# Spreading query and key rows in narrower parts in the last attention layer of a four-layer kernel

## The chip, the cores and the metric

The kernel runs on one core of a Trainium2 chip. The metric is device time of one execution in microseconds (us); less is better. The engines are named as in the profile: PE is TensorE's matmul part and PEld its weight load, DVE is VectorE, ACT is ScalarE, POOL is GpSimd, SP is SyncE, which here only starts DMAs.

## The reference, cut to what matters

A sequence `x` of shape (4, 256, 256) passes through four layers. Each is `x + attention(layernorm(x), ctx)` and then `x + ffn(layernorm(x))`; the context `ctx` has 1601 rows of 256 for each of the four batches. Only the attention of layer 3 is touched, together with the feed-forward that is woven into it:

```python
def _L3_xattn_ref(x, context, Wq, Wk, Wv):        # 32 heads of 8 columns
    q = x @ Wq.T ; kv = interleave(context @ Wk.T, context @ Wv.T)
    q = _rmsnorm(q) ; k = _rmsnorm(k)             # t * rsqrt(mean(t*t) + 1e-6), per head
    attn = softmax(q k^T * 8 ** -0.5)             # 256 queries x 1601 keys, 32 heads
    return attn @ v
x = x + _L3_xattn_ref(_layernorm(x), ctx_2048, ...)
x = x + _L3_ffn_ref(_layernorm(x), ...)           # quantised to whole numbers, 256 -> 1024 -> 256
```

All of it is in float32, except the whole-number matmuls of the feed-forward.

## The kernel before, in words

The program is written engine by engine with Python generators: each `yield` ends a step, and the main loop of layer 3, in `l3`, takes one step of a side generator for each of its own. A scheduler then arranges each engine's instructions, so that the order on an engine is near the program's order, not the same; each engine then works through its instructions in that order.

A head has only 8 columns, so four heads are put on the PE at once, 32 rows apart. For a group `u` of four heads, `runs` (line 1966) takes the transposed rows, copies eight of them to each place by a shuffle on DVE (line 1973), splits the float into low and high bits with two masks on DVE, `hi` (line 1974) and `run` again (line 1975), which also blank the rows that don't belong to the head, and lets POOL subtract them into the matmul operand (line 1976). So a part costs three DVE instructions, in the order shuffle, mask, mask, and one on POOL. `spread` (line 1978) does that for one group: the queries (`qb`, 256 columns) and the keys (`kb`) in parts of 512 columns: 512, 512, 512 and 65. The shuffled rows `run3` have two buffers, the high bits `hi3` one, the operands `qb3` and `kb3` two. There are 8 groups in each of 4 batches: 32 groups, below called heads 0 to 31.

The main loop (from line 2087) goes over batches, groups and 7 pairs of key tiles (six pairs of 128 and one tile of 65 keys). In each step it issues the scores of a pair (8 matmuls, or 4 for the last), their exponentials on ACT (line 2001, two of 128x1024), the value products of the pair before (16 matmuls into the accumulator `o`, which has one buffer), and one step of the side generator `beside`. When a head's last products are done, DVE copies `o` to `os` (line 2103), and the next head's first value products wait for that copy. The spread of the next head begins in step 2 and goes on in steps 3 to 5 of the current one.

`beside` prepares the next batch: `l3_kv` makes keys and values (13 tiles: a matmul `b<-wkv,ctxT`, copies `kr` and `va`), squares and sums them, multiplies the keys by their norms in four products on POOL (line 1739, 4, 4, 4 and 1 tiles), yields three times, and transposes them on the PE (line 1750) into `kT`, which DVE copies (line 1751); `queries` does the same for the queries with squares in `l3_squares` (line 1762, scratch taken from the `run3` buffers). After that it runs the feed-forward of the batch before, in `ffn` (lines 1906 to 1964). All of these PE results go through one PSUM bank (`b`).

Of the kernel before, what the change touches and what calls it, by code (L numbers as in the profile page):

```python
# [24 lines left out]
P = 128  # L25
B = 4
# [34 lines left out]
class Kernel:  # L61
# [1644 lines left out]
    def l3_kv(self, b, st, early):  # L1706


        nc = self.nc
        ctxT = self.ctx3  # L1710
        pool = self.late3 if b % 2 else self.a3
        kr = st["kr"] = self.a3.tile([P, NM, D], F32, name="kr3")
        va = st["va"] = self.va3[b % 2]
        ss = st["ss"] = self.a3.tile([P, (NM + 2) * NH3 + 2], F32, name="ss3")
        for m in range(NM):
            copy = nc.scalar.copy if early() else nc.vector.tensor_copy
            tf = self.take()
            for k in range(2):
                self.mm(tf, ctxT[:, k, m * P : (m + 1) * P], self.wkv3[:, k, :], k == 0, k == 1)
            tp = tf.rearrange("p (h d c) -> p h d c", d=HD3, c=2)  # L1720
            copy(kr[:, m, :].rearrange("p (h d) -> p h d", d=HD3), tp[:, :, :, 0])
            for h in range(2):
                copy(
                    va[h][:, m, : 16 * (HD3 + 1)].rearrange("p (h e) -> p h e", e=HD3 + 1)[:, :, :HD3],
                    tp[:, h * 16 : (h + 1) * 16, :, 1],
                )
            if m in (4, 9, NM - 1):
                m0 = {4: 0, 9: 5}.get(m, 10)
                self.l3_squares(st, kr[:, m0 : m + 1, :], m0, early())
            if m == NM - 1 and b < B - 1:  # L1730
                self.ctx3 = self.load_ctxT(self.a3, b + 1, 1)
            yield
        if b == 0:
            nk = NM * NH3
            self.rstd(ss[:, :nk], ss[:, :nk], 1.0 / HD3, self.eps6)
        for m0, m1 in ((0, 4), (4, 8), (8, 12), (12, NM)):
            v = kr[:, m0:m1, :].rearrange("p m (h d) -> p (m h) d", d=HD3)
            f = ss[:, m0 * NH3 : m1 * NH3, None].to_broadcast([P, (m1 - m0) * NH3, HD3])
            nc.gpsimd.tensor_tensor(v, v, f, ALU.mult)
        yield  # L1740
        yield
        yield
        kT = st["kT"] = [pool.tile([P, MP], F32, name="kT3", bufs=2) for _ in range(2)]
        for m0 in range(0, NM, 4):
            for h in range(2):
                n = min(4, NM - m0)
                copy = nc.scalar.copy if early() else nc.vector.tensor_copy
                tp = self.take().rearrange("p (m k) -> p m k", k=P)
                for m in range(n):
                    nc.tensor.transpose(tp[:, m, :], kr[:, m0 + m, h * P : (h + 1) * P], self.ident)  # L1750
                copy(kT[h][:, m0 * P : (m0 + n) * P], tp[:, :n, :].rearrange("p m k -> p (m k)"))
                yield

    def l3_squares(self, st, v, m0, early, pool=None):

        n = v.shape[1]
        if pool:
            sq = pool.tile([P, 2, D], F32, name="sqq3", tag="run3")
        else:
            sq = self.a3.tile([P, 5, D], F32, name="sq3")  # L1760
        if early:
            self.nc.scalar.activation(sq[:, :n, :], v, AF.Square)
        else:
            self.nc.gpsimd.tensor_tensor(sq[:, :n, :], v, v, ALU.mult)
        self.nc.vector.tensor_reduce(
            st["ss"][:, m0 * NH3 : (m0 + n) * NH3], sq[:, :n, :].rearrange("p m (h d) -> p (m h) d", d=HD3),
            AX.X, ALU.add,
        )

    def l3(self, first):  # L1770
# [11 lines left out]
        with ExitStack() as es:  # L1782
# [37 lines left out]
            def queries(b, st, old=None, fill=lambda n: None):  # L1820

                ss = st["ss"]
                nk, nq = NM * NH3, (NM + 2) * NH3
                if old is not None:
                    stats(old)
                    nc.vector.tensor_scalar(
                        ss[:, nq:], mv[:, old, :, 1], float(HD3), HD3 * (1e-5 - 1e-6), ALU.mult, ALU.add
                    )  # L1830
                elif b:
                    nc.vector.memset(ss[:, nq:], 1.0)
                xn = normed(b, rs[:, b, :])
                fill(0)
                tp = bank().rearrange("p (k q t) -> p k q t", k=2, q=2)
                for k in range(2):
                    for q in range(2):
                        nc.tensor.transpose(tp[:, k, q, :], xn[:, q, k * P : (k + 1) * P], self.ident)
                xT = one.tile([P, 2, S], F32, name="xT3")
                nc.vector.tensor_copy(xT, tp.rearrange("p k q t -> p k (q t)"))  # L1840
                fill(1)
                yield
                tq = bank().rearrange("p (q d) -> p q d", q=2)
                for q in range(2):
                    for k in range(2):
                        self.mm(tq[:, q, :], xT[:, k, q * P : (q + 1) * P], self.wq3[:, k, :], k == 0, k == 1)
                qr = one.tile([P, 2, D], F32, name="qr3")
                nc.vector.tensor_copy(qr, tq)
                self.l3_squares(st, qr, NM, True, two)
                part = ss if b else ss[:, nk:nq]  # L1850
                nc.scalar.activation(part, part, AF.Sqrt, bias=self.eps6, scale=1.0 / HD3)
                nc.vector.reciprocal(ss[:, nk : nq + 2 if b else nq], ss[:, nk : nq + 2 if b else nq])
                qrv = qr.rearrange("p q (h d) -> p (q h) d", d=HD3)
                nc.vector.tensor_tensor(qrv, qrv, ss[:, nk:nq, None].to_broadcast([P, 2 * NH3, HD3]), ALU.mult)
                if b:
                    for c in range(0, nk, nk // 2):
                        nc.vector.reciprocal(ss[:, c : c + nk // 2], ss[:, c : c + nk // 2])
                fill(2)
                yield
                yield  # L1860
                qT = st["qT"] = two.tile([P, 2, S], F32, name="qT3")
                tp = bank().rearrange("p (h t) -> p h t", h=2)
                for h in range(2):
                    for q in range(2):
                        nc.tensor.transpose(tp[:, h, q * P : (q + 1) * P], qr[:, q, h * P : (h + 1) * P], self.ident)
                nc.vector.tensor_copy(qT, tp)
                yield
# [99 lines left out]
            def runs(out, v, u, n):  # L1967

                a = two.tile([P, 512], F32, name="run3")[:, : out.shape[1]]
                t = two.tile([P, 512], F32, name="hi3", bufs=1)[:, : out.shape[1]]
                nc.vector.stream_shuffle(a, v, [8 * u + k % 8 for k in range(32)])  # L1973
                nc.vector.tensor_scalar(t.bitcast(U32), a.bitcast(U32), low[:, n : n + 1], None, ALU.bitwise_and)  # L1974
                nc.vector.tensor_scalar(a.bitcast(U32), a.bitcast(U32), rest[:, n : n + 1], None, ALU.bitwise_and)  # L1975
                nc.gpsimd.tensor_tensor(out, a, t, ALU.subtract)  # L1976

            def spread(st, h, u):
# [1 line left out]
                q = two.tile([P, S], F32R, name="qb3")  # L1980
                k = two.tile([P, MP], F32R, name="kb3")
                yield k, q
                for c in range(0, MP, 512):
                    c1 = min(M, c + 512)
                    runs(k[:, c:c1], st["kT"][h][:, c:c1], u, 0)
                    if c == 0:
                        runs(q, st["qT"][:, h, :], u, 1)
                    yield

            def scores(k, q, ms):  # L1990
# [94 lines left out]
            for b in range(B):  # L2085
                nxt = {} if b else second
                side = beside(b, nxt)
                for n, (h, u) in enumerate(heads):
                    o = ps_o.tile([P, S], F32, name="o3")
                    now = kq  # L2090
                    for c, ms in enumerate(pairs):
                        e = scores(*now, ms)
                        if b + n == 0 and c < 2:
                            for _ in range(c + 1):
                                next(more)
                        if last is not None:
                            values(*last[:6])
                        if done is not None:
# [7 lines left out]
                        else:  # L2106
                            next(side, None)
                        last = (e, o, st["va"], h, u, ms, b)
                        if c == 2:
                            more = iter(())  # L2110
                            if n + 1 < len(heads):
                                more = spread(st, *heads[n + 1])
                            elif b + 1 < B:
                                while "qT" not in nxt:
                                    next(side)
                                more = spread(nxt, 0, 0)
                            kq = next(more, None)
                        if c >= 2:
                            next(more, None)
                for _ in side:  # L2120
                    pass
                st = nxt
# [175 lines left out]
```

## Time and profile before

| | |
|---|---|
| time, three runs | 2550.21 us median (2548.49 to 2553.97) |
| the profiled execution's own time | 2553.43 us |
| its span, first to last instruction | 2551.7 us |
| busy over the span | PE 92%, DVE 62%, ACT 51%, POOL 39% |
| mean granted PE clock over the span | 0.957 |

The loop of layer 3 runs from the first exponential at 1926 us to 2520 us. By batch:

| stretch, us | PE busy | DVE busy | ACT busy | POOL busy | granted clock |
|---|---|---|---|---|---|
| 1926 to 1956 (head 0) | 22.53 | 23.44 | 19.82 | 13.70 | 0.74 |
| 1956 to 2070 (heads 1 to 7) | 101.68 | 73.93 | 85.61 | 42.82 | 0.84 |
| 2070 to 2229 (heads 8 to 15) | 134.28 | 105.14 | 106.02 | 57.21 | 0.96 |
| 2229 to 2395 (heads 16 to 23) | 142.55 | 106.56 | 106.38 | 57.34 | 0.91 |
| 2395 to 2520 (heads 24 to 31) | 112.84 | 66.25 | 101.76 | 37.03 | 0.92 |

How to read it: "busy" of the PE includes matmuls that run slowly. The granted clock is 1.00 or 0.50 at any moment; a mean of 0.84 says that 32% of the stretch ran at half clock. In the lists of waits, a line is the waiting engine with tile and source line, an arrow, the engine and line that ended the wait, and then total us, number of waits and the longest.

### The profile page before, as it was taken

To read this page: it belongs to the slowest core of one execution; us is meant where nothing else is said; L and a number is where in the kernel's file an instruction comes from. 1 tells how busy PE (TensorE), PEld (TensorE's weight loads), DVE (VectorE), ACT (ScalarE), POOL (GpSimd) and SP (SyncE) were. 2 spreads that over 40 slices of the span, in tenths; PEclk is the share of its full clock that TensorE was granted. 3 is DMA by queue.
4 is the path that set the end of the run, shared out by engine and by line. 5 is a ranking of instruction groups with operands and counts; after the bars stand their busy time and mean duration, and the time that the engine had idled before them with its cause. 6 is when DMAs were issued, how large, how long until landed. Compare 5 with 4: busy or idle time off the path is not lost.

```text
span 2551.7 us, 44647 instructions
## 1 busy us (share of the span) xinstructions
PE 2354.8 (92%) x15959; PEld 1434.9 (56%) x15959; DVE 1592.4 (62%) x3552; ACT 1298.8 (51%) x2996; POOL 1005.5 (39%) x1677
## 2 busy tenths in 40 slices
PE   8989997899899999999999999989997888897897
PEld 5778876667545555555555555555553433433443
DVE  5443534843577777777777777763327756657664
ACT  3234444533654545444545454433336766756775
POOL 2015645213355555555555555541114333324330
PEclk9999998989999999999999999998998889998898
DMA  7165675634601111111111111004310100000000
GB/s 254 48 205 165 174 149 169 200 94 139 219 27 48 48 48 48 48 48 48 48 48 48 48 48 48 10 14 164 126 56 28 34 1 28 4 3 2 5 6 5
DMA packets 96516, 188.29 MB, mean 74 GB/s; under 512 B 15449, under 2 KB 64345, under 8 KB 95098
## 3 DMA queue, kind: packets, MB, share of 16 engines
q1 hardware_dynamic: 80150, 146.50, 17.3%
q0 software_dynamic: 10416, 28.46, 4.9%
q10 hardware_dynamic: 5732, 10.49, 1.4%
q8 instruction: 130, 2.13, 0.4%
q14 instruction: 88, 0.72, 0.1%
HBM read 137.29 MB, written 48.11 MB: 73 GB/s over the span
## 4 chain that ended last, share of the span: by engine, by line
PE 70%; DVE 14%; POOL 5%; issue 4%; ACT 3%; DMA 2%; another core or an unknown queue 1%; SPq 0%; ACTq 0%; POOLq 0%; DVEq 0%
PE o L79 21%; PE s L79 18%; PE f2gu L79 3%; POOL kb L1976 3%; PE f1gu L79 2%; PE acc L79 2%; PE tpq L79 2%; PE f0gu L79 2%; DVE run L1973 2%; PE b L79 2%; PE fill L1260 2%; PE tpkv L79 2%; PE av L79 2%; DVE hi L1974 2%; PE f0y L79 1%
## 5 line engine op out<-in xcount | busy, mean ns | idle before, releaser
L1520 ACT ACTIVATE p<-s,nmsm 128x448 f32<-128x448 f32 (+1 forms) x512 | 326.5, 644 | 372.3 <-PE s L79 243.1
L2001 ACT ACTIVATE e<-s 128x1024 f32<-128x1024 f32 (+1 forms) x448 | 398.1, 968 | 172.1 <-PE s L79 171.5
L79 PE MATMUL o<-pT,va 128*128 128x256 f32 (+2 forms) x1920 | 430.2, 376 | 5.9 <-DVE pT L1561 4.3
L79 PE MATMUL s<-kT,qT 128*32 128x448 f32 (+1 forms) x4096 | 427.7, 556 | 7.9 <-ACT kT L1492 7.7
L79 PEld LDWEIGHTS o<-pT,va 128*128 128x128 f32 (+1 forms) x1920 | 344.1, 190 | 126.5 <-issue 86.2
L1555 POOL TENSOR_SCALAR p<-p,rm 128x448 f32<-128x448 f32 (+1 forms) x512 | 324.5, 655 | 6.3
L79 PE MATMUL o<-e,va 128*32 128x256 f32 (+1 forms) x3328 | 291.5, 420 | 19.9 <-DVE os L2103 18.5
L1516 DVE TENSOR_REDUCE nmsm<-s 128x2 f32<-128x896 f32 (+1 forms) x256 | 287.3, 1123 | 8.0
L1561 DVE STREAM_TRANSPOSE pT<-p 128x896 f32<-128x896 f32 (+1 forms) x256 | 270.6, 1110 | 4.8 <-POOL p L1555 4.1
L79 PEld LDWEIGHTS s<-kT,qT 128*32 128x32 f32 x4096 | 120.5, 109 | 259.8 <-issue 238.3
L1976 POOL TENSOR_TENSOR kb<-run,hi 128x512 fp32r<-128x512 f32 (+1 forms) x128 | 137.0, 1070 | 290.9 <-DVE run L1975 154.4
L1548 POOL TENSOR_TENSOR rm<-em,tot 32x8 f32<-32x8 f32 x256 | 54.5, 213 | 396.2 <-DVE tot L1545 384.9
L79 PEld LDWEIGHTS o<-e,va 128*32 128x32 f32 (+1 forms) x3328 | 103.9, 115 | 119.6 <-ACT e L2001 25.4
L79 PE MATMUL s<-qb,kb 32*128 32x256 f32 (+1 forms) x1664 | 133.4, 351 | 16.5 <-ACT e L2001 14.1
L1513 DVE TENSOR_TENSOR s<-s,mask 128x128 f32<-128x128 f32 (+1 forms) x256 | 84.1, 330 | 98.8 <-PE s L79 90.7
L79 PEld LDWEIGHTS s<-qb,kb 32*128 32x128 f32 (+1 forms) x1664 | 78.8, 193 | 112.0 <-issue 72.9
L1974 DVE TENSOR_SCALAR hi<-run,low 128x512 uint32<-128x512 uint32 (+2 forms) x160 | 69.7, 436 | 114.7 <-POOL kb L1976 99.8
L1260 PE MATMUL fill<-wkc_early,ctxT 128*128 128x256 f32 (+1 forms) x444 | 109.6, 398 | 9.0 <-ACT va_early L1268 6.7
L475 POOL DMA_INDIRECT f0xr<-f0xd,f0src x95 | 90.9, 957 | 68.3 <-PE f0y L79 23.6
L1520 ACT ACTIVATION_READ_ACCUMULATOR p<-s,nmsm 128x1 f32 x512 | 101.4, 198 | 0.0
L1260 PEld LDWEIGHTS fill<-wkc_early,ctxT 128*128 128x128 f32 (+1 forms) x444 | 86.3, 198 | 24.9 <-ACT va_early L1268 7.9
L1279 DVE TENSOR_REDUCE ss_early<-sq_early 128x4 f32<-128x512 f32 x64 | 37.0, 579 | 82.2 <-ACT sq_early L1278 64.4
(518 smaller groups left out, 3893.7 us busy)
## 6 DMA issues: line engine op xcount, KB each, us to landing
ctxT<-in_ctxT SPq DMA_DIRECT2D x9, 1664.0 KB
vd<-va_early SPq DMA_DIRECT2D x96, 128.0 KB
kd<-kT_early SPq DMA_DIRECT2D x48, 256.0 KB
kT<-kd SPq DMA_DIRECT2D x16, 768.0 KB
va<-vd SPq DMA_DIRECT2D x16, 768.0 KB
f0yd<-f0ys SPq DMA_DIRECT2D x95, 128.0 KB
wq<-in_l_wq SPq DMA_DIRECT2D x16, 512.0 KB
wo<-in_l_wo SPq DMA_DIRECT2D x16, 512.0 KB
```

The costliest lines, as they stand in the source:

```text
L79: self.nc.tensor.matmul(out, lhsT, rhs, start=start, stop=stop, **kw)
L475: nc.gpsimd.indirect_dma_start(out=t, out_offset=None, in_=xd[:, :], in_offset=bass.IndirectOffsetOnAxis(ap=src[:, n : n + 1], axis=0),)
L1260: ins = nc.tensor.matmul(tp[:rows, t, :], ctxT[u // NKV2][:, k, c0 : c0 + rows], w[u % NKV2][:, k, :], start=k == 0, stop=k == 1,)
L1513: nc.vector.tensor_tensor(sv, sv, mask[:, 2 * c : 2 * c + 2, : nt - CT, :].rearrange("p n t i -> p n (t i)"), ALU.add)
L1516: nc.vector.tensor_reduce(ms[:, 0, 2 * c : 2 * c + 2], s[:, :, : nt * 32], AX.X, ALU.max, negate=True)
L1520: nc.scalar.activation(p[:, n, : nt * 32], s[:, n, : nt * 32], AF.Exp, bias=ms[:, 0, e : e + 1], accum_out=ms[:, 1, e : e + 1],)
L1548: nc.gpsimd.tensor_tensor(r[32 * a : 32 * a + 32], e[:, a], tot, ALU.mult)
L1555: nc.gpsimd.tensor_scalar(p[:, n, : nt * 32], p[:, n, : nt * 32], r[:, e : e + 1], 1.0, ALU.mult, ALU.mult)
L1561: self.pin(nc.vector.transpose(pT[:, 2 * c : 2 * c + 2, :nt, :].rearrange("p n t i -> p n (t i)"), p[:, :, : nt * 32]))
L1974: nc.vector.tensor_scalar(t.bitcast(U32), a.bitcast(U32), low[:, n : n + 1], None, ALU.bitwise_and)
L1976: nc.gpsimd.tensor_tensor(out, a, t, ALU.subtract)
L2001: nc.scalar.activation(e[:kr, :, :n, :], s[t][:kr, :, :n, :], AF.Exp, scale=1.0 / math.sqrt(HD3))
```

## The change

It has four parts, all in layer 3. `spread` handles the queries first and then the keys in parts of 256 columns (six of 256 and one of 65), one in each of the seven steps of the head before, so that it begins in step 0; in the first head its own spread runs along, one part in each step. `run3` and `hi3` become 256 columns wide, with three buffers each. The squares of the queries are taken in two halves. For batches 1 to 3, `l3_kv` yields between its four norm products and once behind them, in place of three times behind them.

```diff
@@ l3_kv
         for m0, m1 in ((0, 4), (4, 8), (8, 12), (12, NM)):
+            if m0 and b:
+                yield
             v = kr[:, m0:m1, :].rearrange("p m (h d) -> p (m h) d", d=HD3)
             f = ss[:, m0 * NH3 : m1 * NH3, None].to_broadcast([P, (m1 - m0) * NH3, HD3])
             nc.gpsimd.tensor_tensor(v, v, f, ALU.mult)
-        yield
-        yield
-        yield
+        for _ in range(1 if b else 3):
+            yield
@@ l3_squares
-        if pool:
-            sq = pool.tile([P, 2, D], F32, name="sqq3", tag="run3")
-        else:
-            sq = self.a3.tile([P, 5, D], F32, name="sq3")
+        sq = pool.tile([P, 1, D], F32, name="sqq3", tag="run3", bufs=3) if pool else self.a3.tile([P, 5, D], F32, name="sq3")
@@ queries
-                self.l3_squares(st, qr, NM, True, two)
+                for q in range(2):
+                    self.l3_squares(st, qr[:, q : q + 1, :], NM + q, True, two)
@@ runs
-                a = two.tile([P, 512], F32, name="run3")[:, : out.shape[1]]
-                t = two.tile([P, 512], F32, name="hi3", bufs=1)[:, : out.shape[1]]
+                a, t = (two.tile([P, S], F32, name=x, bufs=3)[:, : out.shape[1]] for x in ("run3", "hi3"))
@@ spread
-                for c in range(0, MP, 512):
-                    c1 = min(M, c + 512)
+                runs(q, st["qT"][:, h, :], u, 1)
+                for c in range(0, MP, 2 * P):
+                    c1 = min(M, c + 2 * P)
                     runs(k[:, c:c1], st["kT"][h][:, c:c1], u, 0)
-                    if c == 0:
-                        runs(q, st["qT"][:, h, :], u, 1)
                     yield
@@ the main loop, after scores of step c
-                        if b + n == 0 and c < 2:
-                            for _ in range(c + 1):
-                                next(more)
+                        if c == 0:
+                            own = more
+                            more = None
+                            if n + 1 < len(heads):
+                                more = spread(st, *heads[n + 1])
+                            elif b + 1 < B:
+                                while "qT" not in nxt:
+                                    next(side)
+                                more = spread(nxt, 0, 0)
+                            if more is not None:
+                                kq = next(more)
+                        if b + n == 0:
+                            next(own, None)
+                        if more is not None:
+                            next(more)
...
-                        if c == 2:
-                            more = iter(())
...
-                            kq = next(more, None)
-                        if c >= 2:
-                            next(more, None)
```

## The prediction

> **What bounds the kernel now.** Every edit lies in layer 3's loop, 1926 to 2520 us, 18.6 us for each of 32 heads. I read the waits of PE, DVE and POOL in that stretch first:
>
> ```profile
> PE o L79 <- DVE os L2103: 18.5, 16, 2.2
> PE s L79 <- ACT e L2001: 14.1, 15, 3.0
> PE b L1750 <- DVE kT L1751: 13.5, 13, 2.6
> PE b L79 <- DVE va L1723: 8.2, 5, 3.1
> PE b L79 <- DVE g L1938: 6.7, 5, 1.6
> PE b L1750 <- POOL kr L1739: 5.4, 3, 2.6
> ...
> DVE hi L1974 <- POOL kb L1976: 99.8, 92, 5.4
> DVE hi L1974 <- POOL qb L1976: 14.7, 23, 0.8
> ...
> POOL kb L1976 <- PE s L79: 61.9, 15, 12.4
> ```
>
> PE idles 80 us in all, and most of it is for DVE copies. DVE itself stands still 114.5 us in `hi`, since that tile has one buffer and the next mask waits for POOL's subtract; the subtract in turn waits until PE has read the old `kb`. The timeline at the start of head 29 shows how this reaches PE:
>
> ```profile
> 2478.27 0.73 POOL L1976 TENSOR_TENSOR qb<-run,hi 128x256 fp32r<-128x256 f32 x1 [1.36 <-DVE run L1975]
> ...
> 2479.03 0.48 DVE L1974 TENSOR_SCALAR hi<-run,low 128x512 uint32<-128x512 uint32 x1 [0.85 <-POOL qb L1976]
> ...
> 2480.07 0.40 DVE L2103 COPY os<-o 128x256 f32<-128x256 f32 x1
> ...
> 2480.53 1.94 PE L79 MATMUL o<-e,va 128*32 128x256 f32 x16 [1.40 <-DVE os L2103]
> ```
>
> The accumulator was complete at 2478.0, but its copy stood behind a mask that waited for POOL. PE lost 1.40 us and then more, as the busy times by stretch show (the number behind POOL's is the granted clock):
>
> ```profile
> 2476.00:2478.00 2.00, 2.00 (x31) 0.85 (x30) 1.05 (x4) 1.28 (x3) 0.91 (x1) 1.00 0.00 0
> 2478.00:2480.00 2.00, 0.96 (x12) 0.54 (x8) 1.15 (x4) 2.00 (x3) 0.73 (x1) 0.95 0.00 0
> 2480.00:2482.00 2.00, 1.47 (x16) 0.59 (x16) 0.86 (x3) 1.32 (x2) 1.06 (x1) 0.50 0.04 8
> 2482.00:2484.00 2.00, 2.00 (x22) 0.99 (x18) 1.33 (x6) 0.09 (x1) 0.46 (x2) 0.50 0.00 0
> ```
>
> A short wait is followed by half clock. The five stretches of the table by batch make it 2 x (0.26 x 30 + 0.16 x 114 + 0.04 x 159 + 0.09 x 166 + 0.08 x 125) = 115 us at half clock. A pair of key tiles takes 1.9 us at full clock (products start at 2501.62, 2503.52, 2505.35), where ACT's two exponentials of 0.97 us are the limit, and 2.6 us at half (scores at 2483.01 and 2485.60): a microsecond at half clock loses 0.27 us, 31 us in all.
>
> **The parts and their costs.**
>
> *More, smaller parts.* 32 heads x (8 - 5) = 96 more parts: 288 DVE and 96 POOL instructions. By shape DVE's shuffle and masks take 730 + 482 + 483 = 1695 ns for 512 columns, 440 + 353 + 337 = 1130 for 256, 227 + 255 + 244 = 726 for 65. A head goes from 3 x 1695 + 1130 + 726 = 6.94 to 7 x 1130 + 726 = 8.64 us: 1.70 more, 54 us over the loop. POOL goes from 3 x 1.31 + 0.76 + 0.36 = 5.05 to 7 x 0.76 + 0.36 = 5.68, 20 us in all. POOL is busy 208 of 594 us, so its share is hidden. DVE is busy 375; its extra time is hidden where it now stands still (114.5 us), and bare where it is behind. Bounds: 0 and 54. I take 0.2 us a head for 31 heads, 6 us, since DVE had 3.6 us of blocked time per head to give. Without that cover it is the 54.
>
> *Three buffers.* The first wait moves from the second part's mask behind one subtract to the third key part's shuffle behind the queries' subtract. In the changed program's DVE order `os` still stands behind such shuffles: behind that of the sixth part (waiting for the third subtract) in 8 of 31 heads, behind the third to fifth elsewhere. From POOL's start, head 29's copy began at +4.44 us (2475.63 to 2480.07). The new chain is subtracts of 0.73 us, with shuffle, mask, mask between them: +3.9 to +4.3 behind the sixth part, +3.3 behind the fifth, +2.4 behind the fourth. So of the 18.5 us for `os` a third goes, -6; bounds 0 and -18.
>
> *Norm products apart, key transposes later.* In heads 0, 10 and 18 the four products hold POOL for 6.8 to 6.9 us (1739), with the transposes stuck in the middle of a head's products: PE waits 5.4 us for `kr`, then 13.5 us for the `kT` copies, which queue behind masks that wait for subtracts behind those products. In the new order no transpose comes before the third pair of the next head, and two key parts' subtracts go between the products. The `kr` wait goes, -5.4. The copies come at DVE's pace, 3.2 us a pair before (transposes at 2149.93 to 2162.80, four intervals), some 2.7 by my count of the new rows between two copies: -8; bounds 0 and -13.5. The extra `yield` moves transposes, query work and feed-forward one step on; SP's context load is issued with the last key tile, ahead of it, and the output DMAs are not waited for.
>
> *Beside the squares on POOL* (heads 9 and 17) PE waits 3.1 us for `va`. The chain there starts with a subtract of 0.73 instead of 1.28 and one shuffle less: 1.2 us each, -2.4.
>
> *The first head* pays. Its own parts now come one step ahead, and the second stands on DVE behind six adds (line 1169, 2.92 us), the third behind statistics and copies of 4.4 us. Before, one part served two pairs. Adding up the new DVE order I get the last pair 4 us later: +4, bounds 0 and +10. Halved squares add 0.06 us, four times.
>
> *The clock.* If a third of the late copies goes, a quarter of the half clock goes: 115 / 4 x 0.27 = -8; bounds 0 and -20. The Trainium skill, page "TensorE: Matmul & The Clock Gate", Part 1, says that the clock falls after an idle window of about 3.4 us. No wait here is that long, so by it this term is 0 and the sum 8 us smaller; the trace has the fall behind 1.40 us and decides.
>
> The sum: +6 - 6 - 5.4 - 8 - 2.4 + 4 - 8 = -20 us against 2553.4, so 2533.6. The profiled execution is 3.2 us above the median; the forecast for the median is 2530.
>
> **The rivals.**
>
> *DVE and POOL shut each other out* (slower). Before, the single buffer kept masks and subtracts apart; of 320 masks only six met a POOL instruction of over 0.6 us:
>
> ```profile
> 2092.33 2.31 POOL L1764 TENSOR_TENSOR sq<-kr 128x1280 f32<-128x1280 f32 x1
> 2092.40 2.40 DVE L1974 TENSOR_SCALAR hi<-run,low 128x256 uint32<-128x256 uint32 x1 [0.90 <-POOL kb L1976]
> ```
>
> A mask of 0.35 us took 2.40, ending with POOL's instruction. With three buffers, masks and subtracts run side by side. If every subtract holds up one mask for its 0.73 us, a head's DVE time grows by 1.70 + 8 x 0.73 = 7.5, less the 3.6 of waits. DVE now has 375 / 32 = 11.7 busy and 3.6 blocked of 18.6 us: 3.3 free, so 0.6 us a head is bare, 20 us. Of the gains (-30 without the first head) half would go with it: 2550 + 20 + 4 - 15 = 2559. It decides once a head's subtracts hold up masks for more than about 5 us. For it: the row above. Against: shuffles don't meet this (0.739 beside POOL, 0.729 alone), and a held mask waits on average half a subtract. The Trainium skill, "SBUF — State Buffer", section "Who interferes with whom", has the same rule, an exclusive lock between such DVE instructions and GpSimd; the trace agrees.
>
> *The wait only moves* (no change). DVE stops at the third shuffle instead of the second mask, still until PE frees `kb`, and `os` is as late; the clock falls as before. Then -5.4 - 8 - 2.4 + 4 + 6 = -6, and half of the `kT` gain may go too: 2544 to 2552, say 2547. The lower end of my chain (+4.3 against +4.44) speaks for it.
>
> **How the numbers follow.** About 0.2%, 5 us, is what a measurement of this kernel can tell from no change. The forecast case has 0.52, its own range 2512 to 2543; the moved wait 0.20, half of it faster; the shut-out 0.28, almost all slower, to 2575 if it eats all gains. Faster 0.60, same 0.13, slower 0.27. The range, 2508 to 2568, leaves out the far ends of both.
>
> **What would show it.** Right: PE's wait for `kr` gone, those for `os` near 12 and `kT` near 5.5, DVE's waits for POOL well below 114.5, masks of 256 columns near 0.4 on the mean, mean clock in heads 1 to 7 over 0.88, head 0 longer. Wrong: 256-column masks of 0.6 or more on the mean, or `os` waits still near 18.

## The result and the profile after

The changed kernel takes 2524.30 us, median of 4 runs (2522.54 to 2526.93), against 2552.05 us for the kernel before beside it; the ratio is 0.9894 with a 95% interval of 0.9877 to 0.9911. A second comparison, on another chip, gave 0.9893 (0.9875 to 0.9911). So it is faster by 27.8 us, 1.1%, where the forecast was 20 us.

The profiled execution of after took 2525.47 us, with a span of 2523.8 us. Layer 3's loop, from its first exponential to its last, went from 595.3 us (1926.1 to 2521.4) to 565.0 us (1928.7 to 2493.7), 30.3 us less; its later start takes 2.6 us of that back, which is within what the start varies: the other runs in which the layers ahead take as long start it between 1922.8 and 1928.8 us. The same view of both loops (time, then busy us and instructions of PE, PE's weight load, DVE, ACT and POOL, the granted clock, DMA), before first:

```profile
1926.10:2521.40 595.30, 515.17 (x5438) 237.47 (x5436) 375.21 (x1070) 421.00 (x478) 208.10 (x239) 0.90 0.04 12
```
```profile
1928.70:2493.70 565.00, 500.62 (x5438) 237.29 (x5438) 419.17 (x1459) 421.20 (x482) 227.30 (x335) 0.93 0.04 13
```

PE has the same matmuls. It idles 80.1 us before and 64.4 after, 15.7 us less, and is busy 14.6 us less, as it runs fewer of them at half clock (115.9 us of the loop before, 78.5 after, added up from windows of 4 us). These two halves make the 30.3 us. DVE is busy 44 us more (the prediction's sum of durations gave 54) and POOL 19.

These are the waits that the prediction started from, now in after, first PE's and then DVE's (total us, number, longest):

```profile
PE o L79 <- DVE os L2112: 21.1, 17, 2.4
PE s L79 <- ACT e L1998: 11.7, 15, 3.0
PE b L79 <- DVE va L1723: 6.3, 4, 2.4
...
PE b L1751 <- DVE kT L1752: 3.9, 7, 1.2
PE b L79 <- DVE g L1937: 3.2, 7, 1.2
...
PE s L79 <- POOL kb L1974: 2.3, 3, 1.1
```
```profile
DVE run L1971 <- POOL qb L1974: 29.9, 19, 5.7
...
DVE run L1971 <- POOL kb L1974: 9.4, 30, 0.5
```

The wait for `kr` is gone, that for `kT` went from 13.5 to 3.9, `g` from 6.7 to 3.2. DVE's waits for POOL fell from 114.5 to 39.3 us, and stand at the shuffle now. The copy of the accumulator, `os`, did not follow: 18.5 before, 21.1 after.

### The profile page after: what moved, and what is told of

Read it like the earlier page. It is cut to its first block, busy times and chain, and to the rows that moved or that the text cites. A ratio compares the mean times of both kernels' runs of the same rounds, so it can differ in the third digit from the quotient of the medians.

```text
span 2523.8 us, 45207 instructions
## 1 busy us (share of the span) xinstructions
PE 2343.1 (93%) x15959; PEld 1436.2 (57%) x15959; DVE 1635.7 (65%) x3940; ACT 1299.5 (51%) x3000; POOL 1022.5 (41%) x1773
## 4 chain that ended last, share of the span: by engine, by line
PE 75%; DVE 14%; issue 4%; POOL 3%; DMA 3%; ACT 2%; SPq 0%; ACTq 0%; POOLq 0%; DVEq 0%
PE o L79 21%; PE s L79 18%; PE f2gu L79 3%; PE b L79 3%; PE f1gu L79 2%; PE fill L1260 2%; PE f0gu L79 2%; PE acc L79 2%; PE tpq L79 2%; PE tpkv L79 2%; PE av L79 2%; DVE hi L1972 2%; DVE run L1971 2%; PE f0y L79 1%; PE f2y L79 1%
## 5 line engine op out<-in xcount | busy, mean ns | idle before, releaser
L79 PE MATMUL o<-e,va 128*32 128x256 f32 (+1 forms) x3328 | 283.2, 410 | 27.1 <-DVE os L2112 21.1
L1974 POOL TENSOR_TENSOR kb<-run,hi 128x256 fp32r<-128x256 f32 (+1 forms) x224 | 155.8, 707 | 120.8 <-DVE run L1973 119.3
L1972 DVE TENSOR_SCALAR hi<-run,low 128x256 uint32<-128x256 uint32 (+1 forms) x256 | 100.4, 411 | 0.2
L1974 POOL TENSOR_TENSOR qb<-run,hi 128x256 fp32r<-128x256 f32 x32 | 25.9, 810 | 176.4 <-PE s L79 108.4
```

The source lines that it names most:

```text
L79: self.nc.tensor.matmul(out, lhsT, rhs, start=start, stop=stop, **kw)
```

## The experiments

Runs 5 to 7 and runs 8 to 11 were taken on two other chips, where the layers ahead of layer 3 take some 45 us less. So each run is read by its ratio to the kernel before on its own chip, and by its loop. "Half clock" is time of the loop at half clock, worked out as above.

| run | time, us | before beside it | ratio (95%) | loop, us | half clock, us |
|---|---|---|---|---|---|
| before | 2550.2 | | 1 | 595.3 | 116 |
| after | 2524.3 | 2552.1 | 0.9894 (0.9877 to 0.9911) | 565.0 | 79 |
| 1 products apart, alone | 2549.7 | 2552.9 | 0.9983 (0.9974 to 0.9991) | 589.3 | 113 |
| 2 after, products together | 2529.1 | 2552.9 | 0.9900 (0.9883 to 0.9916) | 570.6 | 99 |
| 3 after, old buffer counts | 2563.2 | 2552.9 | 1.0037 (1.0024 to 1.0051) | 601.2 | 113 |
| 4 after, old steps | 2517.1 | 2552.9 | 0.9858 (0.9841 to 0.9875) | 558.7 | 75 |
| 5 after, copy's place fixed | 2509.2 | 2505.5 | 1.0016 (1.0005 to 1.0028) | 597.2 | 126 |
| 6 run 4, copy's place fixed | 2519.6 | 2505.5 | 1.0054 (1.0041 to 1.0066) | 610.1 | 147 |
| 7 before, copy's place fixed | 2539.1 | 2505.5 | 1.0136 (1.0121 to 1.0151) | 623.9 | 160 |
| 8 after again | 2478.9 | 2507.9 | 0.9893 (0.9875 to 0.9911) | 562.5 | 70 |
| 9 after, two accumulators | 2479.4 | 2507.9 | 0.9888 (0.9869 to 0.9907) | 565.2 | 75 |
| 10 run 4, two accumulators | 2472.9 | 2507.9 | 0.9876 (0.9855 to 0.9896) | 560.9 | 82 |
| 11 before, two accumulators | 2508.2 | 2507.9 | 1.0007 (0.9993 to 1.0020) | 591.2 | 106 |
| 12 run 4, copy on ACT | 2524.0 | 2552.2 | 0.9895 (0.9877 to 0.9913) | 570.3 | 86 |

### 1. The norm products alone

```diff
@@ before: l3_kv
         for m0, m1 in ((0, 4), (4, 8), (8, 12), (12, NM)):
+            if m0 and b:
+                yield
...
-        yield
-        yield
-        yield
+        for _ in range(1 if b else 3):
+            yield
```

> The kernel before, with the fourth part of the change alone: the four norm products of the later keys one step apart, parts still 512 columns with two and one buffers. My theory gives this part the waits for the products and for the copies of the transposes: heads 10 to 12 and 18 to 20 were 57.8 and 60.0 us before and 54.4 and 54.5 after, 9 us together. So about 2542 us, 10 below before; the half clock stays near 116 us and DVE's waits for POOL near 110 us. Rival: the whole gain of 28 us comes from here, 2525 us. Other rival: DVE's blocked masks keep the copies late, so that the wait only moves from the products to the copies: 2550 us.

Measured: 3.2 us below before at the median, a loop 6.0 us shorter: between my 10 and the second rival's 2. Its waits of PE:

```profile
PE o L79 <- DVE os L2104: 23.5, 17, 2.4
...
PE b L1751 <- DVE kT L1752: 8.4, 9, 2.3
```

The wait for the products (5.4) is gone and `kT` fell by 5.1, but `os` rose from 18.5 to 23.5. About half of what this part takes away comes back at the copy of the accumulator: "the wait only moves" holds for this part, by half.

### 2. After, with the norm products together

```diff
@@ after: l3_kv
         for m0, m1 in ((0, 4), (4, 8), (8, 12), (12, NM)):
-            if m0 and b:
-                yield
...
-        for _ in range(1 if b else 3):
-            yield
+        yield
+        yield
+        yield
```

> The changed kernel, with the four norm products together again and three steps behind them. My theory: about 10 us above after, 2534 us, with PE's wait for the products back (5 us) and the waits for the copies of the transposes near 8 us; DVE's waits for POOL stay near 40 us outside heads 2, 10 and 18. Rival that all of the gain lies in the products: 2552 us. Rival that the narrow parts with three buffers hide them: 2525 us.

Measured: 2529.1 us, 4.8 us above after by the medians, a loop 5.6 us longer; the intervals of the two ratios overlap, so the time alone does not settle the size. PE's waits do show the exchange:

```profile
PE o L79 <- DVE os L2111: 14.2, 16, 1.6
...
PE b L1750 <- DVE kT L1751: 6.2, 12, 0.8
...
PE b L1750 <- POOL kr L1739: 2.6, 3, 0.9
```

With the products together `os` is 14.2 us. Apart, it is 21.1. So the buffers did shorten the waits for the copy, and the separate products lengthen them again. The timeline of after at the start of head 11 shows where (start, duration, engine and line, what; lines of one kind run together with their number):

```profile
2134.76 6.17 POOL L1741 TENSOR_TENSOR kr<-kr,ss 128x1024 f32<-128x1024 f32 x3 [1.75 <-ACT e L1998]
...
2137.73 3.35 DVE L1972 TENSOR_SCALAR hi<-run,low 128x256 uint32<-128x256 uint32 x2
2138.19 1.08 PE L79 MATMUL o<-e,va 65*32 65x256 f32 x8
...
2141.00 0.81 DVE L1973 TENSOR_SCALAR run<-run,rest 128x256 uint32<-128x256 uint32 x1
2141.73 0.41 DVE L2112 COPY os<-o 128x256 f32<-128x256 f32 x1
...
2142.20 1.08 PE L79 MATMUL o<-e,va 128*32 128x256 f32 x8 [1.97 <-DVE os L2112]
```

Three of the four products still ran back to back (one wait for ACT ahead of the first, none between). Two masks that take 0.7 us together at the median of such masks took 3.35 beside them, and the copy behind those masks was late for it: 1.97 us of PE's time. Heads 1 and 19 show the same, with 2.4 us each. This is the rival that DVE and POOL shut each other out, at three places of the loop and not throughout. The Trainium skill, "SBUF — State Buffer", section "Who interferes with whom", says that a DVE instruction in a two-port mode, which `tensor_scalar` can enter, and GpSimd take a shared port pair in turn, each for its whole instruction; the rows agree: in the single records each of the two masks ends 0.15 us behind one of the products.

### 3. After, with the old buffer counts

```diff
@@ after: runs
-                a, t = (two.tile([P, S], F32, name=x, bufs=3)[:, : out.shape[1]] for x in ("run3", "hi3"))
+                a, t = (two.tile([P, S], F32, name=x, bufs=c)[:, : out.shape[1]] for x, c in (("run3", 2), ("hi3", 1)))
@@ after: l3_squares
-        sq = pool.tile([P, 1, D], F32, name="sqq3", tag="run3", bufs=3) if pool else ...
+        sq = pool.tile([P, 1, D], F32, name="sqq3", tag="run3", bufs=2) if pool else ...
```

> The changed kernel with parts of 256 columns, but two buffers for the shuffled rows and one for the high bits. My theory: the extra DVE work of 54 us is hidden by the blocked time that the third buffer frees; without it DVE waits for POOL in each mask, over 120 us in all (39 after), the copies of the accumulator and of the transposes are as late as before or later, and the half clock is back near 116 us: 2545 to 2555 us, say 2548. Rival: the buffers do nothing, since DVE has 3 us free in each head anyway: 2525 us. Rival that side by side running of masks and subtracts costs more than it brings: masks of 256 columns back at 0.34 us and the time below 2520 us.

Measured: 2563.2 us, more than the 2545 to 2555 I expected, slower than before with its interval above 1, and a loop 36 us longer than after's. Its waits:

```profile
DVE hi L1972 <- POOL kb L1974: 93.9, 146, 0.9
PE o L79 <- DVE os L2112: 28.0, 19, 2.6
...
DVE hi L1972 <- POOL qb L1974: 16.8, 24, 2.1
PE b L79 <- DVE va L1723: 11.4, 9, 2.3
...
PE s L79 <- POOL kb L1974: 8.7, 5, 3.1
```

DVE waits 121 us for POOL in masks and shuffles, as before the change. Most waits of PE are longer: `os` 28.0 against 21.1, `va` 11.4 against 6.3, and that for the key parts `kb` 8.7 against 2.3. Of the 36 us, 30.7 are idle time of PE, and no single wait carries them; PE's busy time is 5.5 us more, though the half clock is back at 113 us. So narrow parts without the buffers cost more than they bring, and the added buffers (one for `run3`, two for `hi3`) are worth more than the whole gain, spread over many waits. More buffers with the wide parts were not tried, so the buffers' worth without the narrow parts stays open. The masks tell the price of running beside POOL (mean ns), first this run and then after:

```profile
L1972 DVE TENSOR_SCALAR hi<-run,low 128x256 uint32<-128x256 uint32 x222 | 86.8, 391 | 95.3 <-POOL kb L1974 77.6 <-POOL qb L1974 16.8
L1971 DVE STREAM_SHUFFLE run<-kT 128x256 f32<-128x256 f32 x190 | 83.7, 442 | 0.0
L1973 DVE TENSOR_SCALAR run<-run,rest 128x256 uint32<-128x256 uint32 x222 | 75.8, 342 | 0.7
```
```profile
L1972 DVE TENSOR_SCALAR hi<-run,low 128x256 uint32<-128x256 uint32 x224 | 91.0, 424 | 0.1
L1971 DVE STREAM_SHUFFLE run<-kT 128x256 f32<-128x256 f32 x192 | 82.7, 442 | 0.0
L1973 DVE TENSOR_SCALAR run<-run,rest 128x256 uint32<-128x256 uint32 x224 | 81.5, 378 | 0.6
```

### 4. After, with the steps of before

```diff
@@ after: spread
                     runs(k[:, c:c1], st["kT"][h][:, c:c1], u, 0)
-                    yield
+                    if c % 512 or c1 == M:
+                        yield
@@ after: the main loop, which becomes that of before
-                        if c == 0:
-                            own = more
...
-                        if b + n == 0:
-                            next(own, None)
-                        if more is not None:
-                            next(more)
+                        if b + n == 0 and c < 2:
+                            for _ in range(c + 1):
+                                next(more)
...
+                        if c == 2:
+                            more = iter(())
...
+                        if c >= 2:
+                            next(more, None)
```

> The changed kernel with parts of 256 columns and three buffers, but issued as before: two key parts in a step, from the third step of the head on (the queries still first), and in the first head its own parts ahead by the old rule. My theory: the steps themselves carry little, because DVE's order is the scheduler's and the copy of the accumulator stands behind the same shuffles; the first head gets back its 4 us: 2518 to 2526 us, say 2521. Rival: one part in each step is what spreads DVE's work evenly, and without it the copies are later by half a microsecond in each head, and the clock falls more often: 2535 us.

Measured: 2517.1 us, just below the 2518 to 2526 I expected and faster than after; the intervals of the two ratios just do not overlap. Heads 0 and 1, first after and then this run (columns as in the loops above):

```profile
1928.70:1961.80 33.10, 23.67 (x168) 10.79 (x172) 28.62 (x92) 19.34 (x22) 13.67 (x15) 0.72 0.15 52
1961.80:1980.40 18.60, 15.97 (x182) 8.44 (x185) 16.88 (x56) 12.62 (x14) 12.13 (x18) 0.77 0.01 2
```
```profile
1927.20:1951.40 24.20, 19.32 (x164) 9.50 (x164) 23.57 (x80) 19.32 (x23) 10.25 (x13) 0.86 0.20 71
1951.40:1972.80 21.40, 17.78 (x186) 9.45 (x186) 20.20 (x63) 12.68 (x15) 15.14 (x18) 0.76 0.01 2
```

The first head is 8.9 us shorter, the second 2.8 longer; that is nearly all of the 6.3 us by which the loop is shorter. In the other heads the steps make no difference beyond the clock: heads 12, 20 and 28 take 13.4, 13.4 and 13.5 us here against 13.3, 13.7 and 13.5. "One part in each step" is a part of the change that costs, in the first two heads.

### 5 to 7. The copy's place on DVE fixed

The same edit in after, in run 4's version and in before: the copy and the shuffles keep the program's order, so the copy stands ahead of the shuffles that wait for POOL.

```diff
-                            nc.vector.tensor_copy(os, last[1])
+                            tc.keep_in_program_order(nc.vector.tensor_copy(os, last[1]))
@@ runs
-                nc.vector.stream_shuffle(a, v, [8 * u + k % 8 for k in range(32)])
+                tc.keep_in_program_order(nc.vector.stream_shuffle(a, v, [8 * u + k % 8 for k in range(32)]))
```

> The changed kernel, with the copy of the accumulator and the shuffles held in the program's order on DVE: the copy then stands behind the first key part of the head after next, not behind its second to fifth. My theory: the step of my prediction that failed is the order, not the wait: the copy stays late (21.1 us of PE waits after, 18.5 before) because shuffles that wait for a subtract stand ahead of it. With the copy ahead of them PE's waits for it fall to about 8 us, and the half clock that follows them (78 us after) to about 40: 13 + 10 us less than after, 2501 us. Rival: DVE reaches the copy no sooner, since the shuffle of the first key part also waits for POOL: 2524 us. Rival: shuffles held back make the key parts late, and PE waits for those instead: 2530 us or more.

> As the run with the steps of before (parts of 256 columns, three buffers, 2517 us), with the copy of the accumulator and the shuffles held in the program's order: the copy then stands ahead of all shuffles of the head after next. My theory: PE's waits for the copy (20.5 us there) fall to about 8 us and half of the half clock goes with them: 2517 - 12 - 9 = 2496 us. Rival that the wait only moves to the key parts, which DVE starts later: 2517 us. Rival that the clock falls for another reason than these waits: the waits go, the half clock stays, 2505 us.

> The kernel before (parts of 512, one buffer for the high bits), with the copy of the accumulator and the shuffles held in the program's order. It separates the copy's place from the buffers. My theory: PE's waits for the copy fall from 18.5 to about 9 us here too and the half clock from 116 to about 80 us, but DVE then does its parts later and stays blocked in the masks, so the copies of the transposes and key parts are later: 2552 - 9 - 10 + 5 = 2538 us. Rival that the copy's place alone gives all that the buffers give: 2520 us. Rival that with one buffer nothing is won: 2552 us.

Measured: all three are slower than the kernel without the edit, by loops that are 35, 49 and 33 us longer (597.2 against run 8's 562.5, 610.1 against run 10's 560.9, 623.9 against run 11's 591.2). For run 7 I had 2538 us and read 2539, but beside a kernel before of 2505.5: the number was met and the theory missed. The waits, of run 5, 6 and 7 in turn:

```profile
DVE r L2018 <- PE b L2015: 25.6, 26, 2.5
...
PE o L79 <- DVE os L2112: 21.1, 20, 4.2
...
PE s L79 <- POOL kb L1974: 15.2, 4, 10.1
```
```profile
DVE r L2019 <- PE b L2016: 37.6, 29, 2.6
...
PE o L79 <- DVE os L2101: 18.4, 15, 3.3
...
PE s L79 <- POOL kb L1974: 13.8, 11, 5.2
...
DVE run L1971 <- POOL kb L1974: 0.3, 1, 0.3
```
```profile
DVE hi L1974 <- POOL kb L1976: 68.5, 70, 1.4
DVE r L2021 <- PE b L2018: 41.4, 24, 2.6
...
PE o L79 <- DVE os L2103: 18.1, 12, 2.6
...
PE s L79 <- POOL kb L1976: 9.7, 7, 1.8
```

In plain heads it did what I expected: head 30 of run 5 takes 13.03 us and has no wait for the copy, against 13.63 and 1.0 us in after. Over the whole loop the waits for `os` did not fall to the 8 or 9 us I expected. DVE now stops soon behind the copy, at `r`, for PE's transposes of it (25.6 to 41.4 us; 5.8 in after), and PE waits for key parts: 15.2, 13.8 and 9.7 us, against 2.3 in after and none in before. That is the rival of run 5, that shuffles held back make the key parts late. In run 5 the first head takes 40.3 us: one of its own key parts stands on DVE behind the norms of the next batch's queries and keys, its masks then run beside the norm products on POOL, and PE waits 10.1 us for it. In runs 5 and 6 DVE hardly waits for POOL in its shuffles, and its waits in all are 127 and 137 us of the loop, against 135 in after. So much the same blocked time, at other places, goes with loops that are 35 and 49 us longer. What fits this is that the cost depends on what stands behind the blocked instruction.

### 8 to 11. After again, and two accumulators

```diff
+            both = ps_o.tile([P, 2, S], F32, name="o3")
             last = done = None
...
-                    o = ps_o.tile([P, S], F32, name="o3")
+                    o = both[:, n % 2, :]
```

> The changed kernel itself, so that the next runs stand beside it on one chip; the layers ahead of layer 3 took 41 to 48 us less in the last three runs than in the others, with the kernel before among them. Its ratio to before was 0.9894; I expect 0.987 to 0.992 here, and its loop of layer 3 at 565 us within 6.

> The changed kernel with two accumulators for the value products, used in turn, in the same place of PSUM; the order of the instructions is the same. PE then need not wait for the copy, however late DVE gets to it. My theory: PE's waits for the copy (21.1 us) go, and the half clock that follows them (78 us in the loop) falls to about 40: heads that lost the wait alone took 13.6 us against 13.0 at ACT's limit, those whose clock fell 15.5; over 17 waits some 20 us in all, ratio to before 0.981. Rival: ACT and the other copies hold PE just as long, ratio 0.989 as for the changed kernel. Rival: the waits go and the half clock stays, ratio 0.984.

> As the run before, in the version with the steps of the kernel before (parts of 256 columns, three buffers, separate norm products; ratio 0.9858): two accumulators. My theory: 0.9858 less some 18 us, 0.979, the fastest of all; the first head stays 7 to 9 us shorter than in the changed kernel. Rival: with the copy's wait gone, PE waits for key parts that DVE makes later in these steps: 0.986.

> The kernel before with two accumulators and nothing else. It tells how much of the change's gain could be had by hiding the late copy alone, with DVE still blocked in its masks for 114 us. My theory: PE's waits for the copy (18.5 us) go and the half clock falls from 116 to about 75 us, 18 us less: ratio 0.993; the waits for the key transposes (13.5) and values (8.2) stay. Rival: DVE's blocked time is the bound and moves the wait to those copies: 1.000. Rival: the late copy was all that the buffers cured: 0.985.

Measured: nothing moved. Run 9's wait stayed:

```profile
PE o L79 <- DVE os L2113: 21.3, 17, 2.4
```

A head's first value product still waits for the last head's copy, though it writes the other half of that PSUM tile. So these three runs did not take the wait away and say nothing of its price; what it is worth stays open, and a second accumulator in a tile of its own was not tried. They serve as repeats: before's loop 591.2 us (595.3), after's 565.2 and 562.5 (565.0), run 4's 560.9 (558.7). So loops of the same instructions differ by some 4 us, and their half clock by up to 10. Run 10 lies 6.1 us below run 8 at the median, as run 4 lay 7.2 below after; here the intervals overlap. But the first two heads repeat: together they take 45.8 us in run 10 and 52.1 in run 8, 45.7 in run 4 and 51.7 in after.

### 12. The copy on ACT

```diff
@@ run 4's version
-                            nc.vector.tensor_copy(os, last[1])
+                            nc.scalar.copy(os, last[1])
```

> The version with the steps of the kernel before (parts of 256 columns, three buffers, separate norm products; ratio 0.9858, and 0.9876 in its repeat with a second accumulator that PE didn't come to use), with the copy of the accumulator on ACT instead of DVE, where it stands behind the first two exponentials of the next head. No shuffle can then hold it up. My theory: PE's waits for the copy (20.5 us over 18, up to 2.0) become 31 short ones of 0.4 to 0.6 us, 15 us, none long enough to be followed by half clock in the plain heads (0.3 to 0.4 us of products for the copy's time); the half clock falls from 75 to 82 us to about 50, and the ratio is 0.981. Rival: ACT sets the pace in most heads (12.1 us of exponentials in 13.0), so that 31 copies of 0.4 us lengthen each head as much as the late copies did: 0.987. Rival: any wait of half a microsecond brings the half clock, which rises to 120 us: 0.995.

Measured: 0.9895, against 0.9858 for run 4. Its waits of PE:

```profile
PE s L79 <- ACT e L1999: 21.8, 35, 3.0
PE b L79 <- DVE va L1723: 6.4, 5, 2.4
...
PE b L79 <- DVE t L2021: 4.1, 3, 1.6
PE b L1751 <- DVE t L2021: 3.2, 4, 1.0
```

PE's waits for `os` are gone, but those for ACT rose from 12.8 to 21.8 us, and PE now waits 7.3 us for `t`, the next step of closing a head (1.1 in run 4). PE idles as long as in run 4, 62 us; the loop is 11.6 us longer by PE's busy time, with the half clock at 86 us against 75. The rival of 0.987 is nearest in its number, but it says that each head grows by ACT's copy, and the heads do not show that. A plain head at full clock takes 13.43 us, 0.2 less than with the late copy on DVE, and heads 1 to 7 together are 4.2 us shorter than in run 4. Heads 12 to 16 and 20 to 24, beside which most of the feed-forward of two batches runs, are 10.7 us longer, and 5.1 of the 7.3 us for `t` are there. Why `t` comes late there was not found out. In head 30, 6.8 us ran at half clock, though its longest wait was 0.5 us.

The fastest version is that of run 4: narrow parts, three buffers and separate products, with the old steps. Its lead over after is 7.2 us in one comparison and within the intervals in the other.

## Why the prediction was right, and where it was not

The sum was -20 us; the median shows -27.8 and the loop of the profiled execution -30.3. By the prediction's own steps:

*Norm products apart, key transposes later* (-5.4 and -8): right at the two waits, -5.4 and -9.6. What it left out is that the products, one by one, still hold DVE's masks and so the copy of the accumulator. Alone, the part brought 3.2 us at the median; in after, undoing it cost 4.8.

*Three buffers* (-6, by a third of the waits for `os`): this step failed as a sum. The waits rose by 2.6 us, and `os` near 18 was my sign of a wrong forecast. Head by head, those that had the wait before went from 18.5 to 13.3 us, and with the products together the total is 14.2, near the 12 I gave. But heads 1, 11 and 19 have 6.8 us that they did not have, behind the masks that the products held, and two others 1.1. Meanwhile the buffers' own worth was far larger than the -6 at `os`: without them the loop is 36 us longer. I priced them at one wait, where without them the waits for `va`, `kT`, `g` and the key parts are longer as well.

*More, smaller parts* (+6, of 54 us of work): no row shows it by itself. The three other parts undone singly cost +36, +5.6 and -6.3 us of the loop; from 565.0 that leads to 600 against 595.3 for before, so about +5 is left for the narrow parts, if the parts add up, which was not tried, and with loops that repeat to some 4 us.

*Beside the squares* (-2.4): in heads 9 and 17 PE's waits for `va` went from 7.6 to 6.3 us, half of what I gave. *The first head* (+4): 29.3 us before, 33.1 after, +3.8; and run 4 shows that the steps cause it.

*The clock* (-8): late copies and half clock do go together by heads. In the 16 heads that had the wait for `os` before, it fell by 28% and the half clock from 65 to 24 us; in heads 1, 11 and 19, where it is new, the half clock rose from 10 to 25 us. Both sizes were too small. The half clock of the loop fell by 37 us where I took a quarter of 115, and a microsecond of it cost about 0.39 us (14.6 / 37.4) where I took 0.27 from the pace of one stretch. Head 29 gives much the same price: 15.04 us in after with 3.4 us at half clock, 13.63 in run 8 with none, 0.41. It is no constant: between after and the other runs whose half clock is 20 us or more longer, the same working gives 0.16 (run 3) to 0.38 (run 7).

*DVE and POOL shut each other out*: the price per mask was small, 0.424 and 0.378 us on the mean against my 0.6 for deciding it, so it did not turn the sign. It was real at the long products. *The wait only moves* held by half for the products alone, and in each of runs 5 to 7, on the copy's place.

So the total came out near with errors of both signs, and that they nearly cancel is luck: the waits for the copy were 8.6 us worse than forecast, the clock 6.6 us better. Of the rest, 6.0 us lay in the waits for `g`, which I had not priced (10.7 to 4.7 us at all its lines), and the +6 for the narrow parts shows as no wait of its own.

## What to carry to other kernels

When an engine works in order and blocks on another, list what stands behind the blocked instruction and price all of it; then a buffer that lets the engine pass is worth more than any one wait shows. Moving a late instruction forward on such an engine can put its successor in the same place: three attempts on one copy each cost more than the copy's 21 us of waits. And a long GpSimd instruction is best kept away from the moment when a DVE mask that others wait for is due, even where the total of such meetings looks small.

## What the runs showed of the hardware

The granted clock changes on a grid of 3.41 us in these traces, and all half clock in the loops comes in such portions. In the loops of the 14 traces here, counted portion by portion with the view of busy times by stretch, PE's busy share in one portion at full clock goes with the clock of the next: below 45% busy, 90 of 92 were followed by half clock; from 85% on, none of 1354; in between, 145 of 510. These are two executions of the same program at the start of head 29, first after and then run 8, with the same wait of 1.00 us for the copy:

```profile
2451.68:2455.09 3.41, 2.42 (x32) 1.05 (x24) 2.90 (x12) 2.68 (x4) 2.65 (x4) 1.00 0.01 2
2455.09:2458.50 3.41, 3.24 (x30) 1.41 (x30) 2.67 (x14) 1.37 (x2) 1.71 (x4) 0.50 0.02 7
```
```profile
2402.85:2406.27 3.42, 2.25 (x30) 1.09 (x30) 2.92 (x14) 3.23 (x4) 2.04 (x3) 1.00 0.03 7
2406.27:2409.68 3.41, 3.41 (x49) 1.72 (x48) 3.14 (x16) 2.83 (x4) 1.91 (x5) 1.00 0.00 0
```

In the first the clock fell, in the second it did not, with PE a little less busy: in this middle range neither the wait nor the busy share of one portion decided the outcome. The prediction had set the Trainium skill's rule ("TensorE: Matmul & The Clock Gate", Part 1: the clock falls after about 3.4 us idle) against the trace. The page also calls the window a free-running one of 3.4 us. That fits the grid, and could be behind the difference between the two executions. The rule quoted names an idle window; here windows in which PE was more than half busy sufficed, as the first pair of rows shows.
